# Query, key and value products of a DiT block by seven products, with the MLP's weight pieces in unused memory

## The chip, the cores and the metric

One core of one Trainium2 chip runs the whole block as one program. The metric is the device time of one execution in microseconds, lower is better; the time before is the median of three runs, 2368.72 us (2368.39 to 2368.92).

The engines are named as the profile names them: PE is TensorE (matrix products; PEld its weight loads), DVE is VectorE, ACT is ScalarE, POOL is GpSimd, and SP is SyncE, which here only issues DMAs. Each engine takes its instructions in the order in which the built program lists them; an instruction that waits holds all behind it on that engine.

## The reference, cut to what matters

A DiT block in fp32 for two sequences ("rows", B=2) of T=2048 tokens, width D=512, 16 heads of 32, hidden width 2048. A condition vector gives six vectors of shift, scale and gate.

```python
mod = silu(condition) @ Wada + bada
sh_a, sc_a, gt_a, sh_m, sc_m, gt_m = split(mod, 6, axis=1)
xm = layernorm(x, g1, be1) * (1 + sc_a) + sh_a
qkv = (xm @ Wqkv).reshape(b, t, 3, H, hd).transpose(2, 0, 3, 1, 4)
scores = einsum("bhqd,bhkd->bhqk", q, k) * hd**-0.5     # causal, softmax
x = x + gt_a * (attn @ Wproj + bproj)
xm = layernorm(x, g2, be2) * (1 + sc_m) + sh_m
x = x + gt_m * (gelu(xm @ W1 + b1) @ W2 + b2)
```

The change concerns the product xm @ Wqkv, and the preparation of W1 and W2 for the MLP.

## The kernel before, in words

**Stages.** In order of time (span of the profiled execution): the query, key and value stage ("Qkv") of row 0 to about 213 us; its attention to 755; its projection to 812, in which the LayerNorm and the transposes of row 1's first tokens are made; the Qkv stage of row 1 from 812 to about 1004; its attention; its projection from about 1546 to 1607; and the MLP of both rows to the end at 2365.

**A Qkv stage** goes over four groups of 512 tokens (`Qkv.group`, L801 on). xmT holds the group's normalised and modulated tokens, transposed: 512 channels as four chunks of 128 partitions, by 512 tokens. For each of four chunks f of 128 outputs, first of the queries and then of the keys, four matmuls (one for each channel chunk, contraction 128, 512 columns; L203) fill one PSUM bank. There are six such banks ("mm"). An fp32 matmul is two passes in the trace. The scores of the attention need a query or key as a high part and a residue, both fp32r: ScalarE writes the scaled high part, hl[:,0] (L821), VectorE the residue hl[:,1] = scaled product − hl[:,0] (L822), and SyncE stores both to DRAM in one DMA of 512 KB (L827). hl has four buffers in row 0, three in row 1. After f=0 the four key loads and four query loads of the group (256 KB each, L305 to L325) follow on SyncE; kst is one tile for all four groups. Then come four value tiles: four matmuls of 512 columns each, copied by ScalarE (L843) into vv, which stays on chip.

**What is put between.** After each of the twelve output tiles, `between(n)` issues the rest: the load of the next group's x (n=0), its LayerNorm and transposes (n=5 and 8: VectorE normalises into xn, L244; TensorE transposes, L211; VectorE modulates even chunks, L263, and ScalarE odd ones, L268), and `also(g, n)`. Within the matmuls `among` brings scores of the attention's first three units forward in groups 1 to 3: TensorE fills one of two banks "s", VectorE takes the row maximum (L461, or L456 where the causal mask applies).

**What sets the order.** Instructions wrapped in `mm()` or `act()` stay in program order; the tile scheduler may move the others. All DMAs of `nc.sync` go through SyncE's queue in order, and with at most eight outstanding there. In row 0, `also` loads the modulation's weights ("wada", L1050): for two of the six vectors at a time, eight DMAs of 256 KB on SyncE, in group 0 and in group 1.

**The MLP's weights.** The MLP already multiplies by seven products in place of eight (a form of Strassen's scheme, with halves of contraction, outputs and tokens), which needs sums of weight blocks. `Quarters` (L876 to L950) makes them during the Qkv stages, all on GpSimd: it issues the loads of a piece of W1 or W2 (L929, L942), adds blocks (L913) and stores the piece to DRAM (L902). There are eight W1 pieces (seven blocks of 128x256: four sums) and four W2 pieces (eight sums, of 512 and 896 columns, then seven stores). Their memory is that of wada in row 0 and a tile of its own in row 1.

Of the kernel before, what the change touches and what calls it, by code (L numbers as in the profile page):

```python
# [27 lines left out]
def dit_block_kernel(  # L28
# [119 lines left out]
    rstd2 = const.tile([P, B * NT], F32, tag="rstd2", name="rstd2")  # L148
    shift2 = const.tile([P, B * NT], F32, tag="shift2", name="shift2")
# [70 lines left out]
    def inv_std(mv, rstd, lo, hi):  # L220
        nc.scalar.activation(rstd[:, lo:hi], mv[:, lo:hi, 1], AF.Sqrt, bias=eps)
        nc.vector.reciprocal(rstd[:, lo:hi], rstd[:, lo:hi])

# [6 lines left out]
    def transposed(pool_, psum, xts, n0, mv, rstd, a, c, b, dst, xns=None):  # L230
# [28 lines left out]
        def modulate(chunks=range(C)):  # L259
            for k in chunks:  # L260
                src = banks[k // per][:, k % per, :]
                if k % 2 == 0 and not by_act:
                    nc.vector.tensor_scalar(  # L263
                        dst[:, k, :], src,
                        a[:, k, b : b + 1], c[:, k, b : b + 1], ALU.mult, ALU.add,
                    )
                else:
                    nc.scalar.activation(  # L268
                        dst[:, k, :], src, AF.Identity,
                        bias=c[:, k, b : b + 1], scale=a[:, k, b : b + 1],  # L270
                    )
# [17 lines left out]
    class Row:  # L289
# [18 lines left out]
        def load_keys(self, c, g, n=1):  # L308

            tok = slice(g * MT, (g + n) * MT)  # L310
            if g == 0:
                self.kst[c] = self.pools[c % 2].tile(
                    [P, HC, T], F32R, tag=f"kst{c % 2}", name="kst"
                )
            for r in range(4):
                nc.sync.dma_start(
                    self.kst[c][r * HD : (r + 1) * HD, :, tok].bitcast(F32),
                    kd[self.b][c][r % 2, :, tok].rearrange("(h d) t -> d h t", d=HD),
                )
# [65 lines left out]
        def prefetch(self):  # L385
# [6 lines left out]
            st = bp.tile([P, HC, T], F32R, tag="kst0", name="kst")  # L392
            st = st.bitcast(F32).rearrange("p h t -> p (h t)")
            self.at_s = [
                st[:, n * C * QB : (n + 1) * C * QB].rearrange("p (c q) -> p c q", c=C)
                for n in range(2)
            ]
            self.xt_s = [st[:, (2 * C + n) * QB : (2 * C + n + 1) * QB] for n in range(TQ)]
            self.wproj = st[:, 3 * C * QB :].rearrange("p (c d) -> p c d", c=C)
# [42 lines left out]
        def bank(self, u, h, t, kb, s):  # L442
# [6 lines left out]
                self.kst[c][:, h, kb * QB : kb * QB + w],  # L449
# [86 lines left out]
    def attention_phase(row):  # L536
        b, vv, kst, qst = row.b, row.vv, row.kst, row.qst
        with pool(f"att{b}") as ap, pool(
# [6 lines left out]
            def scores_t(u, step, n):  # L545
# [29 lines left out]
                for h in range(HC):  # L575
                    at = 0
                    for j, q in tiles:
                        mm(
                            sts[h][:, at : at + QB - q],
                            kst[c][:, h, j * P : (j + 1) * P],  # L580
# [178 lines left out]

    class Qkv:  # L760


        def __init__(self, row, qp, psum):
            self.row, self.qp, self.psum = row, qp, psum
            self.xts, self.xmT = {}, {}
            self.w = qp.tile([P, C, 3 * D], F32, tag="wqkv", name="wqkv")
# [9 lines left out]
        def load_w(self, queue):  # L776
            w_v = Wqkv.rearrange("(c p) f -> p c f", p=P)
            for f in range(0, 3 * D, D):
                act(queue.dma_start(self.w[:, :, f : f + D], w_v[:, :, f : f + D]))

        def stats(self, g, t, keep=False):
# [3 lines left out]
            if t == MTT - 1:  # L785
                inv_std(mv1, rstd1, n0, n0 + MTT)

        def norm(self, g, j):

            b = self.row.b  # L790
            if j == 0:
# [3 lines left out]
                self.xmT[g] = self.qp.tile([P, C, MT], F32, tag="xmT", name="xmT", bufs=2)  # L795
            return transposed(
                self.qp, self.psum, self.xts[g][2 * j : 2 * j + 2],
                b * NT + g * MTT + 2 * j, mv1, rstd1, a1, c1, b,
                self.xmT[g][:, :, j * 2 * P : (j + 1) * 2 * P],
            )  # L800

        def group(self, g, hp, between, among):


            row, w, psum = self.row, self.w, self.psum
            b, xmT = row.b, self.xmT[g]
            tok = slice(g * MT, (g + 1) * MT)
            n = 0
            for f in range(C):
                for which in range(2):  # L810
                    ps = psum.tile([P, MT], F32, tag="mm", name="ps_qk")
                    w0 = which * D + f * P
                    for k in range(C):
                        mm(
                            ps, w[:, k, w0 : w0 + P], xmT[:, k, :],
                            start=(k == 0), stop=(k == C - 1),
                        )
                        among(n, k)
                    hl = hp.tile([P, 2, MT], F32R, tag="hl", name="hl", bufs=4 - b)
                    scale = HD**-0.5 if which == 0 else 1.0  # L820
                    nc.scalar.activation(hl[:, 0, :], ps, AF.Copy, scale=scale)  # L821
                    nc.vector.scalar_tensor_tensor(  # L822
                        hl[:, 1, :], ps, scale, hl[:, 0, :].bitcast(F32),
                        ALU.mult, ALU.subtract,
                    )
                    dst = (qd if which == 0 else kd)[b][f]
                    nc.sync.dma_start(  # L827
                        dst[:, :, tok].rearrange("l p t -> p l t"), hl.bitcast(F32)
                    )
                    between(n)  # L830
                    n += 1
                if f == 0:
                    row.load_keys(0, g)
                    row.load_queries(g)
            for t in range(MTT):
                ps = psum.tile([P, D], F32, tag="mm", name="ps_v")
                for k in range(C):
                    mm(
                        ps, xmT[:, k, t * P : (t + 1) * P], w[:, k, 2 * D : 3 * D],
                        start=(k == 0), stop=(k == C - 1),  # L840
                    )
                    among(n, k)
                nc.scalar.copy(row.vv[:, g * MTT + t, :], ps)  # L843
                between(n)
                n += 1

        def run(self, hp, also):

            row = self.row
            for g in range(NG):  # L850

                def between(n):
                    if g + 1 < NG:
                        if n == 0 and g + 1 not in self.xts:
                            self.load_x(g + 1)
                        if n in (5, 8):
                            self.norm(g + 1, n // 8)()
                    elif n == 8:

                        row.rows(0)  # L860
                        act(nc.scalar.activation(first, eps, AF.Exp))
                    also(g, n)

                def among(n, k):
                    if g > 0 and n >= 2:


                        past = 4 * (n - 2) + k + 1
                        if g == 1:
                            row.score(row.count(cum[0] * past / 40, 0))  # L870
                        else:
                            past += 40 * (g - 2)
                            row.score(
                                row.count(
                                    cum[0] + (cum[2] - cum[0]) * past / 80,
                                    1 if g == 2 and n < 7 else 2,  # L876
# [3 lines left out]
                self.group(g, hp, between, among)  # L880

    w1_v = W1.rearrange("(c p) f -> p c f", p=P)
    w2_v = W2.rearrange("(c p) f -> p c f", p=P)

    piece = 7 * C // 2 * P
    S1, S2, A11, S4, A12, A22, S3 = range(7)
    A21 = S4

    class Quarters:

# [5 lines left out]
        def __init__(self):  # L896
            self.rooms, self.more_rooms, self.at = [], None, 0
            self.to = []

        def store(self):  # L900
            for dst, w in self.to:
                nc.gpsimd.dma_start(dst, w)  # L902
            self.to = []

        def sums(self, part):

            for n, x, y, op in (
                (S1, A21, A22, ALU.add),
                (S3, A11, A21, ALU.subtract),
                (S2, S1, A11, ALU.subtract),  # L910
                (S4, A12, S2, ALU.subtract),
            ):
                nc.gpsimd.tensor_tensor(part(n), part(x), part(y), op)  # L913

        def step(self):

            self.store()
            f, self.at = self.at, self.at + 1
            if f >= FC // 2 + C:
                return  # L920
            if not self.rooms:
                self.rooms = self.more_rooms()
            w = self.rooms.pop(0)
            base = ((A11, 0, 0), (A12, 0, 1), (A21, 1, 0), (A22, 1, 1))
            if f < FC // 2:
                w = w[:, :piece].rearrange("p (n c d) -> p n c d", n=7, d=P)
                for n, i, k in base:
                    at = (f + i * FC // 2) * P
                    nc.gpsimd.dma_start(  # L929
                        w[:, n],  # L930
                        w1_v[:, k * C // 2 : (k + 1) * C // 2, at : at + P],
                    )
                self.sums(lambda n: w[:, n])
                self.to = [(w1d[f], w)]
                return
# [803 lines left out]
```

## Time and profile before

| | |
|---|---|
| Median of three runs | 2368.72 us (2368.39 to 2368.92) |
| Profiled execution: time, span | 2366.88 us, 2365.2 us |
| Granted TensorE clock | 1.000 |
| Qkv stage, row 0: groups | 17.9 to 60.98 to 108.56 to 162.79 to about 213 us |
| Qkv stage, row 1: groups | 812.2 to 855.3 to 902.3 to 953.7 to about 1004 us |
| Busy VectorE in row 0's groups | 12.9, 21.5, 35.8, 30.8 us |
| Busy GpSimd in row 1's groups | 27.1, 27.4, 30.8, 18.5 us |

The profile gives one execution. Its first part has the busy time of each engine. The chain is the work that ended last, followed back from the end, each step to what released it; in order of time it shows runs of one kind of instruction with their start and length. Groups of instructions show engine, output and inputs, shape, count, then busy time, mean of one in ns, and the idle time before them with its releaser. A window of a stage lists the busy time of each engine in it. A stretch of SyncE's queue shows when DMAs were issued. The mean of a matmul in a group (594 ns) counts ends that overlap the next; what one adds to the chain is read from the chain.

### The profile page before, as it was taken

Reading aid. Unit: us, or ns where it says so; the run is one execution under the profiler, and the core shown is the slowest. Engines: PE = TensorE matmul, PEld = TensorE weight load, DVE = VectorE, ACT = ScalarE, POOL = GpSimd, SP = SyncE. Lnnn points to the kernel's source line nnn. Section 1 sums busy time; section 2 is a strip of 40 time slices with the busy share of each in tenths; the row PEclk is TensorE's granted clock in tenths of the full one; section 3 lists DMA queues with packets and bytes.
Section 4 is the critical chain, followed back from the end, with each engine's and each line's share of the span. In section 5 each row is a group of like instructions: output and inputs, shape, how many; then the busy total and the mean of one; then the engine's idle time right before and its main releaser. Section 6 shows DMA issues by size and latency. Waiting matters only on the chain.

```text
span 2365.2 us, 32348 instructions
## 1 busy us (share of the span) xinstructions
PE 2336.9 (99%) x11469; PEld 1294.6 (55%) x11469; DVE 1397.6 (59%) x2868; ACT 924.1 (39%) x1736; POOL 1079.2 (46%) x1219
## 2 busy tenths in 40 slices
PE   8999999999999999999999999999999999999998
PEld 4455555555544445555555555444585486487477
DVE  3466666767656636576666766553483374365356
ACT  2113555555555012155555555613322332332321
POOL 1052997978793646379887997460000000000000
PEclk9999999999999999999999999999999999999999
DMA  7577215151223788650513214272254254353433
GB/s 258 188 249 195 49 28 118 27 117 46 83 106 132 255 259 259 220 113 24 117 46 85 59 31 144 78 252 100 98 170 146 94 179 139 119 166 132 135 124 129
DMA packets 134106, 311.49 MB, mean 132 GB/s; under 512 B 14208, under 2 KB 29100, under 8 KB 129080
## 3 DMA queue, kind: packets, MB, share of 16 engines
q1 hardware_dynamic: 126096, 277.13, 38.9%
q0 software_dynamic: 7472, 31.75, 3.7%
q8 instruction: 90, 1.47, 0.3%
q14 instruction: 72, 0.59, 0.1%
q10 hardware_dynamic: 376, 0.55, 0.1%
HBM read 229.95 MB, written 87.29 MB: 134 GB/s over the span
## 4 chain that ended last, share of the span: by engine, by line
PE 96%; DVE 2%; POOL 1%; issue 0%; DMA 0%; ACT 0%; SPq 0%; POOLq 0%; ACTq 0%; DVEq 0%
PE st L203 20%; PE ps_a L203 17%; PE o L203 11%; PE s L203 10%; PE ps_qk L203 9%; PE ps_b L203 9%; PE ps_v L203 5%; PE ps_o L203 5%; PE ps_c L203 4%; PE sm L203 4%; PE ps_xt L211 1%; POOL ee L614 1%; PE ps_o L211 1%; DVE mx L461 0%; DVE junk L456 0%
## 5 line engine op out<-in xcount | busy, mean ns | idle before, releaser
L586 ACT ACTIVATE e<-st 128x512 f32<-128x512 f32 (+1 forms) x1152 | 574.6, 578 | 428.1 <-PE st L203 361.6
L614 POOL TENSOR_TENSOR ee<-ee,e 128x512 f32<-128x512 f32 x424 | 529.2, 1289 | 4.4 <-ACT e L586 4.0
L461 DVE TENSOR_REDUCE mx<-s 128x1 f32<-128x512 f32 x604 | 407.9, 688 | 204.5 <-PE s L203 203.1
L203 PE MATMUL s<-kst,qst 128*128 128x512 f32 (+3 forms) x1032 | 463.7, 451 | 5.7 <-DVE mx L461 2.9
L203 PE MATMUL st<-qst,kst 128*128 128x512 f32 (+3 forms) x1280 | 409.4, 387 | 0.0
L203 PE MATMUL ps_a<-sum,w 128*128 128x256 f32 (+1 forms) x1088 | 346.6, 454 | 0.0
L203 PE MATMUL o<-e,vv 128*32 128x512 f32 (+3 forms) x2560 | 300.5, 538 | 2.0 <-POOL e L592 2.0
L456 DVE CUSTOM_DVE_ANT_0 junk<-s,causal 128x512 bf16<-128x512 f32 (+3 forms) x428 | 209.3, 489 | 135.5 <-PE s L203 127.6
L203 PEld LDWEIGHTS s<-kst,qst 128*128 128x128 f32 x1032 | 194.4, 189 | 155.7 <-DVE mx L461 55.6
L203 PEld LDWEIGHTS st<-qst,kst 128*128 128x128 f32 x1280 | 227.3, 188 | 94.2 <-issue 62.2
L203 PEld LDWEIGHTS ps_a<-sum,w 128*128 128x128 f32 x1088 | 206.3, 190 | 109.8 <-issue 91.4
L614 POOL TENSOR_TENSOR ee<-e 128x512 f32<-128x512 f32 x168 | 210.4, 1285 | 101.4 <-ACT e L586 101.0
L203 PE MATMUL ps_qk<-xmT,wqkv 128*128 128x512 f32 x512 | 239.0, 594 | 1.8 <-DVE xmT L263 1.8
L592 POOL TENSOR_SCALAR_AFFINE_SELECT e<-e 128x128 f32<-128x128 f32 (+1 forms) x384 | 122.4, 357 | 135.0 <-ACT e L586 132.3
L203 PE MATMUL st<-fold,sel 32*128 32x512 f32 (+1 forms) x1152 | 149.1, 481 | 0.9 <-ACT vv L843 0.5
L203 PEld LDWEIGHTS ps_qk<-xmT,wqkv 128*128 128x128 f32 x512 | 93.9, 190 | 97.0 <-issue 90.4
L1318 DVE TENSOR_TENSOR h<-c,ps_b 128x512 f32<-128x512 f32 x32 | 22.0, 687 | 202.4 <-PE ps_b L203 202.4
L203 PEld LDWEIGHTS st<-fold,sel 32*128 32x128 f32 x1152 | 59.3, 181 | 144.8 <-ACT e L586 86.6
L203 PE MATMUL ps_v<-wqkv,xmT 128*128 128x512 f32 x256 | 122.3, 594 | 0.0
L203 PE MATMUL ps_b<-sum,w 128*128 128x256 f32 (+1 forms) x384 | 120.6, 450 | 0.0
L203 PEld LDWEIGHTS o<-e,vv 128*32 128x32 f32 x2560 | 61.1, 108 | 102.0 <-issue 81.0
L1492 ACT ACTIVATE h<-h,cols 128x512 f32<-128x512 f32 x96 | 69.2, 721 | 118.6 <-DVE h L1318 118.6
(155 smaller groups left out, 2601.3 us busy)
## 6 DMA issues: line engine op xcount, KB each, us to landing
qst<-q SPq DMA_DIRECT2D x128, 256.0 KB
w<-w1d SPq DMA_DIRECT2D x32, 896.0 KB
w<-w2d SPq DMA_DIRECT2D x28, 1024.0 KB
kst<-k SPq DMA_DIRECT2D x24, 1024.0 KB
w<-w2d SPq DMA_DIRECT2D x28, 768.0 KB
q<-hl SPq DMA_DIRECT2D x32, 512.0 KB
k<-hl SPq DMA_DIRECT2D x32, 512.0 KB
w2d<-w POOLq DMA_DIRECT2D x28, 448.0 KB, 6.5
```

The costliest lines, as they stand in the source:

```text
L203: return tc.keep_in_program_order(nc.tensor.matmul(*args, **kw))
L211: return tc.keep_in_program_order(nc.tensor.transpose(dst, src, ident[:n, :n]))
L456: nc.vector.tensor_tensor_reduce(junk[:, :w], s[:, :w], causal[:, QB - w :], 1.0, MASKED, ALU.add, ALU.max, m,)
L461: nc.vector.tensor_reduce(m, s[:, :w], axis=AX.X, op=ALU.max)
L586: act(nc.scalar.activation(e[:, :w], sts[h][:, :w], AF.Exp))
L592: nc.gpsimd.affine_select(d, d, pattern=[[0, len(tiles)], [1, P]], compare_op=ALU.is_ge, fill=0.0, base=0, channel_multiplier=-1,)
L614: act(engine.tensor_tensor(dst, x, y, ALU.add))
L1318: act(nc.vector.tensor_tensor(dst, x, y, ALU.add))
L1492: nc.scalar.activation(d, ps, AF.Gelu, bias=col(r_b1 + half * HF + f, 1))
```

## The change

**Queries and keys by seven products.** For a group and an f, the query chunk and the key chunk are the two halves of the outputs (i = 0, 1), channel chunks 0-1 and 2-3 the halves of the contraction, and tokens 0-255 and 256-511 the halves of the tokens. The four products of halves come from seven block products, each two matmuls of 256 columns; the weights and tokens of four of these are sums (S1 to S4). Banks a, b and c collect them:

```diff
+            return [
+                step("a", A11, True, first, 0, 0),
+                step("b", S1, True, first, 1, 1),
+                step("a", S2, False, first, 0, 1),
+                step("b", S4, False, last, 0, 1),
+                step("c", A12, True, last, 0, 0),
+                step("a", S3, False, last, 1, 1),
+                step("a", A22, False, direct, 1, 0),
+            ]
```

`first` copies a bank into hl[:,1] on ScalarE (128x256), `last` adds a bank to it on VectorE, and `direct` is a copy that completes the key. The last step of a unit is issued after the second of the next unit:

```diff
+                    for step in steps[:2] + late + steps[2:6]:
+                        step()
+                        tick()
+                    late = steps[6:]
```

Then the chunk is split into high part and residue, on ScalarE and GpSimd, before SyncE stores it:

```diff
-                    hl = hp.tile([P, 2, MT], F32R, tag="hl", name="hl", bufs=4 - b)
-                    nc.scalar.activation(hl[:, 0, :], ps, AF.Copy, scale=scale)
-                    nc.vector.scalar_tensor_tensor(
-                        hl[:, 1, :], ps, scale, hl[:, 0, :].bitcast(F32),
-                        ALU.mult, ALU.subtract,
-                    )
...
+                hp.tile([P, 2, MT], F32R, tag="hl", name="hl", bufs=4) for _ in range(2)
...
+            def split(i):
+                hl = hls[i]
+                d = hl[:, 1].bitcast(F32)
+                nc.scalar.copy(hl[:, 0], d)
+                nc.gpsimd.tensor_tensor(hl[:, 1], d, hl[:, 0].bitcast(F32), ALU.subtract)
+                self.stored(g, f, i, hl)
```

**Values** are two units a group by the same seven products with the same token sums: the tokens are the weights of TensorE there, the value weights' seven blocks (256 columns) move; `first` and `last` copy and add into vv. A group is thus six units of seven products, and `tick` is called after each product (42 a group). Only unit (0, 0) of row 0 is computed as before (`plain`).

**Sums.** Token sums S1, S2, S3 (ticks 36, 38, 40 of the group before) and A22 (tick 2) are VectorE operations of 128x512 in place in xmT or in three new tiles. Weight sums of queries and keys: GpSimd in row 0, sixteen of 128x256; in row 1 three of 128x1024 on VectorE and one on GpSimd, during the projection. Value weights: four of 128x512 on GpSimd, in each row's first group (tick 10 in row 1).

**LayerNorm.** xn is now made by ScalarE in place in the x tile, with a new vector `shift1`, and modulation is ScalarE's too, but for row 0's first group. x of the next group is loaded at tick 3; its norm is at ticks 18 and 28.

**MLP pieces** (`Pieces` for `Quarters`): loads go through SyncE's queue; sums and stores are queued and taken by ticks, on GpSimd still; the memory is that of vv, kst and qst that is not used yet. `plan(f, room, load, start)` gives the ticks, counted through the stage:

```diff
+        def tick(self):
+            for f in self.events.pop(self.at, ()):
+                f()
+            self.at += 1
+            for _ in range(2 if len(self.ops) > 12 else 1):
+                if self.ops:
+                    self.ops.pop(0)()
...
+        pieces.plan(FC // 2, room_2, 5, 17)
+        for f, (room, load, start) in enumerate((
+            (room_v, 4, 12), (room_v, 25, 36), (room_v, 46, 54), (room_k, 56, 63),
+            (room_q, 66, 73), (room_k, 80, 87), (room_q, 91, 98), (room_k, 105, 112),
+        )):
+            pieces.plan(f, room, load, start)
...
+            for f, (room, load, start) in enumerate((
+                (room_2, 0, 6), (room_1, 16, 24), (room_2, 39, 46),
+            ), FC // 2 + 1):
+                pieces.plan(f, room, load, start)
```

Row 0 so takes one W2 piece and the eight W1 pieces, row 1 the other three W2 pieces. A W2 piece in `room_2` lies in four parts of memory, so its eight sums are twenty operations: four of 512 columns, twelve of 256, four of 128; the seven stores are one step, taken by one tick.

**Other moves.** wada has its memory in vv; its eight DMAs in group 0 are issued at tick 7. kst is a tile for each group, so the attention's key loads of 1 MB become four of 256 KB each. The MLP's computation is not changed.

## The prediction

> **What bounds the kernel now.** I read the page's busy row first, then the shares of the chain, then the costliest groups.
>
> ```profile
> PE 2336.9 (99%) x11469; PEld 1294.6 (55%) x11469; DVE 1397.6 (59%) x2868; ACT 924.1 (39%) x1736; POOL 1079.2 (46%) x1219
> PE 96%; DVE 2%; POOL 1%; issue 0%; DMA 0%; ACT 0%; SPq 0%; POOLq 0%; ACTq 0%; DVEq 0%
> ...
> L203 PE MATMUL ps_qk<-xmT,wqkv 128*128 128x512 f32 x512 | 239.0, 594 | 1.8 <-DVE xmT L263 1.8
> ...
> L203 PE MATMUL ps_v<-wqkv,xmT 128*128 128x512 f32 x256 | 122.3, 594 | 0.0
> ```
>
> TensorE is busy 99% of the span and carries 96% of the chain, at a granted clock of 1.00 everywhere: work taken off it is time gained, unless it then waits. The two lines are the passes that the change touches, 512 + 256 = 768 (two for each fp32 matmul). Their mean, 594 ns, is the modelled end of overlapping passes; the chain in order of time gives what one costs:
>
> ```profile
> 812.22 20.60 PE ps_qk L203 x48
> ...
> 860.66 4.55 DMA x<-in_x_dram
> ```
>
> 48 passes in 20.60 us are 0.429 each. A pass of 256 columns costs 0.216 (the MLP's seven products: 8 in 1.73 us, in the same view), so halving the columns halves the cost. The second line is the only stall: in the second group of batch row 1 the next group's x landed late and TensorE stood for 1.2 us. So the present order has much cover, and the question is how much of it the change uses up. The busy times of the stages tell it (us, PE, PEld, DVE, ACT, POOL, clock, DMA share, GB/s); first two groups of row 0, then of row 1:
>
> ```profile
> 17.90:60.98 43.08, 43.05 (x112) 20.00 (x113) 12.91 (x27) 11.12 (x20) 0.16 (x1) 1.00 0.70 224
> 60.98:108.56 47.58, 47.58 (x146) 22.61 (x144) 21.54 (x62) 9.75 (x18) 0.00 (x0) 1.00 0.65 210
> ...
> 812.20:855.30 43.10, 43.10 (x114) 19.97 (x113) 15.37 (x32) 8.90 (x18) 27.08 (x32) 1.00 0.82 271
> 855.30:902.30 47.00, 45.78 (x129) 22.16 (x128) 22.88 (x59) 9.02 (x17) 27.35 (x27) 1.00 0.84 264
> ```
>
> GpSimd does nothing in row 0's first two groups and 27 us in row 1's. No query, key or value waits for it anywhere, since it only makes MLP weight pieces. That is what the change gives up.
>
> **TensorE's gain.** A group is 96 passes now, 96 × 0.429 = 41.2 us. After: six units of seven products, each two matmuls of two passes, 168 × 0.216 = 36.3: −4.9. The very first unit stays plain (16 × 0.429 + 140 × 0.216 = 37.1): −4.1. Over eight groups 7 × 4.9 + 4.1 = **−38.2 us**, if nothing waits.
>
> **Vector and scalar engines.** VectorE loses, a group, eight residues (0.687), four normalisations (0.55) and four modulations (0.54), and gains 18 adds of 256 columns (0.42, the MLP's rows) and four token sums (0.61, half of the 1.22 for 1024 columns): −0.2 us, so 13 to 36 us of a group as before. ScalarE goes to about 22 us of 39 to 49. Both are covered. What may not be is order: a late operation ahead of an add in VectorE's queue holds TensorE (it does, below).
>
> **GpSimd.** Its rates:
>
> ```profile
> L913 POOL TENSOR_TENSOR w<-w 128x256 f32<-128x256 f32 x32 | 23.2, 735 | 10.6 <-DMA w<-in_L_cond_W_dram 9.5
> ...
> L913 POOL TENSOR_TENSOR w<-w 128x512 f32<-128x512 f32 x16 | 20.2, 1264 | 19.4 <-DMA w<-in_L_cond_W_dram 18.6
> L902 POOL DMA_DIRECT2D w2d<-w x28 | 15.2, 548 | 1.2 <-POOL w L913 1.2
> ```
>
> Start to start they are 0.72 and 1.22, a store's issue 0.55. After the change the residue of each query and key chunk (the split, 128x512, 1.22) is taken on this engine, eight a group, in program order behind whatever the ticks have queued. A tick is one product, 4 × 0.216 = 0.86 us: each tick that queues a sum of 1.22, or two operations while more than twelve stand, puts GpSimd further behind. A split that is late makes its store late, the store frees one of four hl tiles, and the next unit's first product can't be copied out without a tile; its PSUM bank takes the third product, so TensorE stops there, two or three products later. From a store's issue to the load that depends on it SyncE's queue shows 3.4 to 6.1 us (26.59 to 30.0, 172.04 to 178.18).
>
> A W2 piece costs GpSimd four sums of 512 (4.9), twelve of 256 (8.6), four of 128 (0.5 each, below the 256 row: 2.0) and seven stores (3.9): 19.4 us, where the sums went in eight wider operations before. Row 1 adds three such pieces in its first two groups (58.2), 16 splits (19.5), the value weights' sums (4.9) and loads (4 × 0.72): **85.5 us**, starting 3.5 us in. TensorE's own work there is 36.3 + 1.7 of transposes, and 2.9 of scores more in the second group: 38 + 41 = 79 us; it took 90.1 before. So in these two groups GpSimd is the busier engine, and the splits stand in its line. Walking the queue in program order from 812.1: the second unit's splits end at T+24.8 and T+29.5, and with 4 us for a store to land the waits at third and fourth products are 3.5 + 4.9 + 3.8 = 12 us; the third piece, begun four ticks into the next group, gives 5.6 + 2.0 = 7.5. The bounds: 0 (tiles are never short, as now) and 24 (6.1 us to land, everywhere).
>
> **Row 0, first group.** Two waits, one inside the other. First SyncE:
>
> ```profile
> 34.37 0.38 SPq L827 DMA_DIRECT2D q<-hl  x1
> 34.79 5.86 SPq L1050 DMA_DIRECT2D wada<-in_L_cond_Wada_dram  x6
> 41.45 0.38 SPq L827 DMA_DIRECT2D k<-hl  x1
> ```
>
> The key chunk, ready at 33.3, was stored at 41.45 because six loads of modulation weights stood ahead, 0.98 us each; there were tiles to spare. Now the second unit's query store stands behind all eight, and loads of MLP pieces are on this queue as well (they were on GpSimd's): issued about 44, landed 47 to 50, where the fourth unit wants the tile at 37.8: some 10 us. Second, GpSimd: from 18.1 us, 29 sums of 256 (20.9), 8 sums and 4 splits of 512 (14.6) and four issues (2.2) stand up to the store of W2's third part: 55.8 us. It lands 6.5 later (the median of the 28 in the page's DMA list, 2.8 to 13.3), at 62.3; a W1 load into the same memory waits for it on SyncE's queue, with two loads of the next group's x behind it; these land near 66, and their statistics stand ahead of the fifth unit's value adds on VectorE. TensorE goes on at about 68.4 with 5.3 us to do: the group ends at 73.7 instead of 60.98 − 4.1 = 56.9. **+16.8**; it is 13 with a landing of 2.8, 24 with 13.3, and 0 if pieces and x never meet.
>
> The Trainium skill ("DMA: Bandwidth & Descriptors", Anatomy of one DMA — SWDGE path) has a store as a fixed 2.0 us and its bytes at 436 GB/s: 3.1 us for 448 KB, against 6.5 here, where several queues move at once. By the page this group's wait would be 13.4, and the sum 3.4 us lower.
>
> **Row 0, second group.** The eight modulation loads took 83.01 to 91.2 on SyncE; a key store again comes behind them and one unit later there is no tile: 6.5 us (0 to 10).
>
> **Third and fourth groups.** W1 pieces only (3.4 us each), GpSimd at a third: no wait taken, 0 to 3 a row.
>
> **Attention, projection, MLP.** Sixteen key loads of 256 KB in place of four of 1 MB, on a queue with long gaps there; six operations on VectorE in projection 0 under TensorE's 57 us. Taken at nothing; without that cover 1 to 3 us.
>
> VectorE and GpSimd at once:
>
> ```profile
> L244 DVE TENSOR_SCALAR xn<-x,mv,rstd x28: 534/545/2301, 7.6 to 928.1; 128x512 f32<-128x512 f32 x28
> ...
> L244 DVE TENSOR_SCALAR xn<-qst,mv,rstd x12: 514/1008/4846, 773.8 to 1592.2; 128x512 f32<-128x512 f32 x12
> ```
>
> (min/median/max): 0.55 alone, up to 4.8 beside GpSimd. These go to ScalarE, but four token sums a group come, and the splits run beside them; 0 to 1 us each on the way to the next group, taken at nothing. "SBUF — State Buffer", Who interferes with whom, says that an operation with two SBUF inputs and a reading GpSimd lock each other out entirely: by it the token sums would lose a split's length each, some 1.2 us, 30 us over the kernel if none were covered; no row here shows that form.
>
> **Sum.** −38.2 + 16.8 + 6.5 + 12 + 7.5 = **+4.6 us**. The profiled execution took 2366.88 (span 2365.2), so 2371.5 by it; on the median of 2368.72, 2373.3. Forecast: **2373 us**. A measurement of this kernel tells 0.2% (4.7 us) from no change.
>
> **Rivals.**
> - *The waits are half as long*: stores land in 3 us, SyncE's modulation loads go out faster since half of the bytes asked for then are gone from GpSimd's queue, and the walk stacked waits that overlap. 21 us of waits, −17: about 2352. For it: stalls that I added one after another; every late store of before (41.45, 91.31) did no harm. Against: four tiles with two taken by each unit.
> - *Nothing waits*: 2368.72 − 38.2 = 2330.5. The 1.2 us stall in all of before's eight groups speaks for it; GpSimd's 85.5 us in 79 against it.
> - *Slower, by GpSimd's line alone*: if its operations are stretched by VectorE at its side (the split's row may go from 1.22 to 1.48, as the slowest 128x512 group on that engine shows), row 1's two groups hold 85.5 × 1.15 = 98 us, 8 to 13 more, and row 0's first 6 more: about 2390. It decides as soon as GpSimd's work in those groups exceeds TensorE's by more than the four tiles hold, one unit, 6 us.
>
> **How the numbers follow.** Waits of 36 to 50 us (2366 to 2380) 0.41; half 0.27; nothing 0.08; slower by GpSimd's line 0.24. Of the first case a half lies within 0.2%. Faster 0.36, same 0.20, slower 0.44. Range 2344 to 2393: both bounds of the row 0 landing and the half case lie in it; all of the gain doesn't. The likeliest case alone: 2366 to 2380.
>
> **What would show it.** In the changed kernel's profile: 1316 passes of 256 columns at 0.216; the first group ending near 73, the groups at 812 near 50 us each, with TensorE's idle time released by the copy into hl (ScalarE), behind it a store; GpSimd near 85 us of those two groups; the last two groups of each row 5 us shorter. If the first group ends before 61, or the pair at 812 takes under 85, the waits are smaller than worked out and the kernel is faster; if GpSimd's 128x512 rows exceed 1.4 us, it is slower.

## The result, and the profile after

The changed kernel takes 2426.82 us (median of 4 runs, 2425.97 to 2428.19) against 2368.82 (4 runs): a ratio of 1.0245, 95% interval 1.0227 to 1.0263. It is 58 us slower, where no change to speak of was forecast, and outside the range.

The busy row, the shares of the chain and the granted clock, from the page of the changed kernel:

```profile
PE 2326.1 (96%) x12033; PEld 1413.6 (58%) x12033; DVE 1404.1 (58%) x2930; ACT 1009.9 (42%) x1952; POOL 1147.5 (47%) x1291
...
PEclk9899999999999988999999999999999999999999
...
PE 82%; DMA 5%; POOL 5%; issue 3%; DVE 2%; SPq 1%; ACT 1%; POOLq 0%; DVEq 0%; ACTq 0%
```

TensorE's busy time fell by only 11 us, its share of the chain from 96% to 82%, and DMA, which held nothing of the chain, now holds 5%. The clock dips twice, in the slices of the two Qkv stages. Span by span (us):

| | before | after |
|---|---|---|
| up to the first query product | 17.9 | 19.5 |
| Qkv stage, row 0 | 194.5 | 220.7 |
| attention 0 | 542.4 | 542.0 |
| projection 0 | 57.2 | 58.6 |
| Qkv stage, row 1 | 191.2 | 221.4 |
| the rest, to the end of the span | 1361.9 | 1362.5 |

Of the 59.5 us in span, 56.4 lie in the two stages, which should each have become 19 us shorter if nothing waited. The windows of their first two groups (columns as in the prediction: us, PE, PEld, DVE, ACT, POOL, clock, DMA share, GB/s; row 0, then row 1):

```profile
19.50:79.90 60.40, 41.43 (x168) 31.11 (x169) 22.79 (x46) 23.85 (x50) 51.42 (x64) 0.89 0.92 304
79.90:138.60 58.70, 46.67 (x218) 38.74 (x217) 21.92 (x67) 20.38 (x45) 20.94 (x24) 0.85 0.73 244
```

```profile
840.80:904.40 63.60, 47.15 (x181) 38.41 (x180) 15.57 (x38) 20.07 (x45) 55.58 (x67) 0.84 0.76 249
904.40:964.10 59.70, 47.37 (x201) 40.39 (x200) 20.76 (x66) 20.27 (x45) 28.86 (x36) 0.83 0.60 204
```

TensorE stands idle 12 to 19 us in each, and what it does runs at a mean clock of 0.83 to 0.89. Who held it is read from one operation, the copy of a bank into an hl tile on ScalarE (L938): what ScalarE waited for before it, and which engine then waited for the copy (us, times). The second view is of the kernel before: who waited for its stores of queries and keys.

```profile
its engine sat idle before it (us, times) until:
...
  DMA q<-hl: 27.2, 8
  DMA k<-hl: 24.5, 9
...
who waited for it (us, times):
...
  PE ps_a L204: 37.6, 10
...
  PE ps_b L204: 18.8, 5
```

```profile
L827 SPq DMA_DIRECT2D k<-hl x32: 359/377/863, 26.6 to 996.7; - x32
...
who waited for it (us, times):
  ACT hl L821: 4.0, 1
```

ScalarE's copies stood 51.7 us for stores, where they stood 4.0 before, and TensorE stood 56.4 us for the copies: TensorE waits for the copy, the copy for a tile, the tile for a store.

### The profile page after: what moved, and what is told of

It reads as the page before. It is cut to its first block, busy times and chain, and to the rows that moved or that the text cites. A ratio compares the mean times of both kernels' runs of the same rounds, so it can differ in the third digit from the quotient of the medians.

```text
span 2424.7 us, 34152 instructions
## 1 busy us (share of the span) xinstructions
PE 2326.1 (96%) x12033; PEld 1413.6 (58%) x12033; DVE 1404.1 (58%) x2930; ACT 1009.9 (42%) x1952; POOL 1147.5 (47%) x1291
## 4 chain that ended last, share of the span: by engine, by line
PE 82%; DMA 5%; POOL 5%; issue 3%; DVE 2%; SPq 1%; ACT 1%; POOLq 0%; DVEq 0%; ACTq 0%
PE ps_a L204 20%; PE st L204 19%; PE o L204 11%; PE ps_b L204 10%; PE s L204 9%; PE ps_c L204 5%; PE sm L204 4%; PE ps_o L204 3%; DMA k<-hl 2%; DMA q<-hl 1%; POOL kst L1123 1%; POOL hl L944 1%; PE ps_xt L212 1%; POOL ee L621 1%; DVE mx L468 1%
## 5 line engine op out<-in xcount | busy, mean ns | idle before, releaser
L204 PE MATMUL s<-kst,qst 128*128 128x512 f32 (+3 forms) x1032 | 419.1, 410 | 6.8 <-DVE mx L468 6.3
L944 POOL TENSOR_TENSOR hl<-hl 128x512 fp32r<-128x512 f32 x62 | 78.8, 1270 | 198.8 <-ACT hl L943 166.6
L468 DVE TENSOR_REDUCE mx<-st 128x1 f32<-128x512 f32 x164 | 112.6, 687 | 4.1 <-PE st L204 1.3
L204 PE MATMUL ps_a<-t,wqk 128*128 128x256 f32 x248 | 67.2, 400 | 39.3 <-ACT hl L938 37.4
```

Of the source, the lines that this page charges most:

```text
L204: return tc.keep_in_program_order(nc.tensor.matmul(*args, **kw))
L468: nc.vector.tensor_reduce(m, s[:, :w], axis=AX.X, op=ALU.max)
L944: nc.gpsimd.tensor_tensor(hl[:, 1], d, hl[:, 0].bitcast(F32), ALU.subtract)
```

## The experiments

Row 0 and row 1 below are the lengths of the two Qkv stages; idle is TensorE's in each (from the waits in its queue). Times are of one run, but for the first two kernels and six; the kernel before took 2367.7 to 2368.4 on the same chips.

| | time | row 0 (idle) | row 1 (idle) |
|---|---|---|---|
| before | 2368.8 | 194.5 (0) | 191.2 (1.2) |
| changed | 2426.8 | 220.7 (35) | 221.4 (32) |
| split_vector | 2422.8 | 229.2 (38) | 208.5 (27) |
| wada_spread | 2423.4 | 217.0 (28) | 219.8 (33) |
| comb | 2409.3 | 218.4 (29) | 206.5 (25) |
| comb2 | 2409.7 | 212.4 (22) | 210.6 (26) |
| wv_four | 2427.5 | 219.2 (31) | 224.0 (39) |
| wv_seven | 2394.5 | 203.3 (17) | 205.1 (27) |
| spare_only | 2405.8 | 207.5 (22) | 213.0 (33) |
| fix | 2408.0 | 216.5 (27) | 206.2 (25) |
| wv_seven_x | 2360.8 | 192.5 (11) | 184.2 (10) |
| wv_seven_all | 2359.9 | 186.6 (3) | 188.0 (11) |
| x_ahead | 2420.0 | 219.9 (34) | 214.6 (29) |
| mixed | 2405.2 | 216.4 (24) | 203.3 (17) |
| six | 2370.7 | 197.9 (12) | 187.5 (10) |
| old_two | 2386.8 | 199.9 (4) | 205.0 (10) |

### The two queues that the prediction named

**split_vector:** the residue is made on VectorE.

```diff
-                nc.gpsimd.tensor_tensor(hl[:, 1], d, hl[:, 0].bitcast(F32), ALU.subtract)
+                nc.vector.tensor_tensor(hl[:, 1], d, hl[:, 0].bitcast(F32), ALU.subtract)
```

> Theory A (GpSimd's line): the split of a query or key chunk stands in GpSimd's queue behind the MLP pieces' sums, so its store, and with it the hl tile that the next unit's first copy wants, comes late. With the split on VectorE, nothing of a query or key waits for GpSimd: row 1's Qkv stage goes from 221 to about 185 us, row 0's (where SyncE's modulation loads hold the stores as well) from 221 to about 212, the time from 2427 to about 2382. Theory B (the seven-product form itself: more copies, adds and one chain over two banks, whoever makes the residue): the stages keep their length within 10 us, 2417 to 2437, since VectorE gets 8 x 0.69 us a group more.

Measured: 2422.8, in the range of theory B. Row 1's stage became 13 us shorter where theory A had 36, and row 0's 8.5 longer. GpSimd no longer touches a query or key, and the copies still wait 48.8 us for stores (51.7 in the changed kernel). Theory A is a part of row 1's loss, not the whole. Some stores of row 1 now stood on SyncE; this is the one behind the longest wait there (SyncE's queue, and two pieces of the chain):

```profile
918.70 4.12 DMA k<-hl
...
922.84 4.51 SPq L319 DMA_DIRECT2D kst<-k  x4
...
930.14 8.17 DMA q<-hl
```

A query chunk was ready at 921.4 us, but its store was issued at 930.1: ahead of it on SyncE stood the attention's key and query loads, and the first key load waited for the group's first key store to land. TensorE then waited 8.4 us for that tile. No run moves these loads, so what they cost is open.

**wada_spread:** the modulation loads one at a time.

```diff
...
+            if todo and n % 3 == 0:
+                todo.pop(0)()
```

> The sixteen modulation loads of row 0 are issued one at a time, every third tick, in place of eight at once. Theory C (SyncE's line): in row 0's first two groups the stores stand behind the eight loads (10.3 and 11.6 us of SyncE); without them the 15.3 us wait in the first group goes to under 5 and the 4.5 and 7.5 us waits in the second to under 3; row 0's Qkv stage goes from 221 to about 198 us, row 1's stays at 221, the time is about 2404. If only GpSimd's line counts (theory A alone), row 0's stage stays above 215 and the time above 2420.

Measured: 2423.4, with row 0's stage at 217.0, the signs that were named for GpSimd's line alone. The 15.3 us wait of the first group went to 9.0, but a wait of 1.6 us for a value add became 6.8; the waits on stores went from 51.7 to 40.9. Theory C missed by 19 us.

**comb**, both, with `g < 2` choosing VectorE, and **comb2**, with the W2 piece of row 0 a group later:

> Both edits, with the split on VectorE in the first two groups of a row and on GpSimd in the last two. Theories A and C together: row 0's stage about 185 us, row 1's about 183, no wait on a store over 2 us, granted clock 1.00, time about 2352. If the waits have a further source (DMA bandwidth in row 0's first group, share 0.92; order on ScalarE), one of the stages stays above 195 us and the time above 2365.

> As the kernel with both edits, and the W2 piece of row 0 is moved from the first group to the second (its loads at tick 38, its sums from tick 46), with the W1 pieces behind it. If the W2 piece's loads, stores and sums in the first group still cost something after the other two edits, row 0's stage is 3 to 8 us shorter than there; if not, the two agree within 2 us.

Measured: 2409.3 and 2409.7; waits on stores in comb still 42.6 us. comb gains more than the sum of the two alone (17.5 us against 7.5; the split is on GpSimd again in the last two groups here), and is 57 short of what both theories together promised. In comb2 row 0's stage is 6.0 us shorter than in comb, as was expected if the W2 piece costs something there; but row 1's stage, whose code is the same in both, is 4.1 longer, and the times agree. A stage with the same code can so differ by 4 us, and single gains of that size in the table show little. The two queues are then a part of the loss, 17.5 of 58 us: with one late link mended, the next took its place. What they all feed is the hl tile, and the next runs ask whether it has too little slack.

### Tile life

**wv_four** and **wv_seven** leave out the value weights (the value products read the query weights, so the values are not the reference's) and so free memory; only the second gives it to hl:

```diff
     def load_wv(self, hp, queue):
-            self.wv = hp.tile([P, 7, HK, D // 2], F32, tag="wv", name="wv")
...
+            self.wv = self.w[:, :, :, : D // 2]
...
-                hp.tile([P, 2, MT], F32R, tag="hl", name="hl", bufs=4) for _ in range(2)
+                hp.tile([P, 2, MT], F32R, tag="hl", name="hl", bufs=7) for _ in range(2)
```

> Control. The value weights' tile, its loads and its sums are left out: the value products read the query weights instead, so the values are not those of the reference; the work on TensorE, VectorE and ScalarE is the same, GpSimd loses 4.9 us a row and SyncE four loads. hl keeps four tiles. Every theory: between 2412 and 2425 us, the waits of ScalarE's first copy on stores (51.7 us in the changed kernel) above 40.

> The same with the memory so freed given to hl: seven tiles in place of four, nothing else. Theory D (tile life): in the changed kernel an hl tile is taken at a unit's first product and is the place where products are added up, so it is held through a unit (6 to 8 us) before its store starts; four tiles are two units, which leaves about 4 us for the split, SyncE and the landing, and every store that takes longer is a wait of TensorE. With seven tiles the waits on stores fall from 50 to under 12 us, the granted clock in the stages rises to 0.97 or more, and the time is 50 to 70 us below the control, about 2355. Theory B (the form itself, or engines in the unit's chain): within 15 us of the control, above 2400.

Measured: 2427.5 and 2394.5. The control lies 2.5 us above its range and within 1 us of the changed kernel; its copies wait 39.6 us for stores. Three tiles more are worth 33 us. TensorE's waits in row 1's stage and its surroundings (total, times, longest), wv_four and then wv_seven:

```profile
PE ps_a L204 <- ACT hl L929: 27.1, 5, 9.8
PE ps_b L204 <- ACT hl L929: 6.5, 2, 4.9
PE ps_a L204 <- ACT vv L1000: 4.8, 1, 4.8
```

```profile
PE ps_xt L212 <- ACT x L844: 19.8, 4, 17.4
PE ps_a L204 <- ACT hl L929: 4.6, 1, 4.6
PE ps_a L204 <- DVE vv L1004: 2.9, 2, 2.3
```

The waits on hl go from 33.6 us to 4.6; in both stages together ScalarE's copy no longer lists a store of queries or keys among its releasers. But more than half of that is given back at once: a wait of 17.4 us for the transposes of the next group's x appears, and the gain is short of the expected 50 to 70 us. TensorE now gets ahead of x, and x is late by two things. Its loads landed at 892.5 us, 5.4 after TensorE stopped; then a VectorE instruction on the way to the normalisation, of 0.17 us in the median, took 9.28:

```profile
894.32 9.28 DVE L224 SCALAR_TENSOR_TENSOR shift<-mv,rstd 128x4 f32<-128x4 f32 x1
...
901.63 1.94 POOL L1114 TENSOR_TENSOR qst<-qst 128x256 f32<-128x256 f32 x4
```

All that time GpSimd ran one operation on on-chip tiles after another, and both ended at the same moment, 903.6 us. This points to VectorE being held by GpSimd; no run shows it by taking GpSimd's work away.

**old_two:** the kernel before with two tiles.

```diff
-                    hl = hp.tile([P, 2, MT], F32R, tag="hl", name="hl", bufs=4 - b)
+                    hl = hp.tile([P, 2, MT], F32R, tag="hl", name="hl", bufs=2)
```

> The kernel before with two hl tiles in each row in place of four and three, nothing else. There a tile is held for the two halves (0.60 + 0.69 us) and its store; a chunk comes every 3.4 us, so two tiles leave some 5.5 us for a store against 15 and 10 now. Theory D: stores of 4 to 8 us then hold the copies, and with six PSUM banks in between TensorE waits some, 5 to 40 us over both stages, 2374 to 2410. If a store's wait does not reach TensorE: within 4 us of 2368.

Measured: 2386.8, +18 us, within the expected range. ScalarE's copies waited 72.4 us for stores, 27 times, more than in the changed kernel, and TensorE was idle 14 us against 67: so there a store's wait reaches TensorE much less. From the program, the reason would be that a chunk is complete in its bank and six banks stand between, while in the seven products the third product needs the first one's bank back; no run tests that by itself.

### x, with and without tiles

**wv_seven_x** adds to wv_seven, and **x_ahead** to the changed kernel:

```diff
...
+                        if n == 30 and g + 2 < NG:
+                            self.load_x(g + 2)
+                        if n in (8, 10, 12, 14) and g + 1 > row.b:
+                            self.stats(g + 1, (n - 8) // 2, True)
+                        if n in (15, 25):
+                            self.normalise(g + 1, n // 25)
```

> The kernel with the value weights left out (values not the reference's) and seven hl tiles, and x earlier: the next group's x is loaded at tick 30 of the group before in place of tick 3, its statistics are held in program order at ticks 8 to 14, its normalisation is issued three ticks ahead of the transposes. Theory E (x's line): with tiles to spare, what is left are waits of TensorE for transposes of an x that is late on SyncE, and for adds that stand on VectorE behind its statistics, 17.4 + 6.2 + 3.2 + 2.3 + 1.8 + 1.5 us in the kernel with seven tiles. They go: time 2352 to 2368. Theory B (the form itself): within 10 us of 2394.

> The changed kernel (full computation, four tiles) with x earlier as there, nothing else. Theory D: tiles bound it first, so the time falls by the waits on value adds alone (1.6 + 5.9 us) or less: 2412 to 2425. If x's line is the main cause, it falls by 30 us or more, below 2397.

Measured: 2360.8 and 2420.0, both as theories E and D had them. The same edit is worth 34 us with seven tiles and 7 with four. Theory B, that the form itself is slow, is out: with tiles and an early x it runs 8 us below the kernel before. The edit also moves the statistics to another time, and no VectorE instruction is held for 9 us any more, so the 34 us are not divided between x's loads and GpSimd's hold. **wv_seven_all** (with comb's two edits) asks for the rank of the queues:

> The same, with the split on VectorE in the first two groups of a row and the modulation loads one at a time. Theories A and C as lesser causes that seven tiles cover: within 8 us of the kernel without these two edits, either way. If GpSimd's and SyncE's lines still hold stores back: 10 to 20 us less, 2340 to 2350.

Measured: 2359.9, no difference from wv_seven_x: with tiles to spare, the split's engine and the modulation loads cost nothing in sum (row 0's stage is 5.9 us shorter, row 1's 3.8 longer). **fix** and **spare_only**, the full computation with eight tiles in the first two groups, came too early for this:

> Full computation. In the first two groups of a row every second unit takes its two hl tiles from the key memory of the third and fourth group, which is unused then: eight tiles there. The MLP pieces leave that memory: row 0 makes the eight W1 pieces only, row 1 the four W2 pieces. Split on GpSimd, modulation loads eight at once. Theory D: the waits on stores in the first two groups fall to a third, those of the last two groups stay (1 to 3 us each); time 2365 to 2395. If GpSimd's and SyncE's lines are what counts (theories A and C), it stays above 2400.

> Eight hl tiles in the first two groups as there, and the split on VectorE in those groups, the modulation loads one at a time, and the statistics of the next group's x kept in program order, so that on VectorE they no longer stand ahead of the value adds (waits of 1.6 to 6.8 us there). Theory D with A and C as lesser causes: both Qkv stages between 175 and 186 us, granted clock 0.99 or more, time 2335 to 2350, below the kernel before. Theory B: above 2395.

Measured: 2405.8 and 2408.0; both missed, and on the side of the other theories. spare_only won 21 us, 11 less than its range asks, and lies above the 2400 named for theories A and C. One wait is more than that difference: at 951.9 us TensorE had stood 16.9 us for a tile. On SyncE a load of the next W2 piece had waited 18.8 us for the store of the piece before it from the same memory, with stores of keys and queries behind it. So eight tiles do not cover a queue that is held that long. fix lies 58 us above its range, where theory B was expected. In it, statistics were put in order at the tick of the transposes themselves; TensorE waited 5 to 7 us for x five times (43.2, 91.4, 145.1, 900.3 and 958.1 us), and row 0's third query load waited for a piece stored from its memory. These waits are 30 us, and some 40 with the 1.9 us lost after each (an estimate from the rows further down): most of the miss is that edit's, as far as can be told without a run that takes it back alone.

**mixed** gives tiles their room in another way:

> Full computation: queries and keys by seven products, values plain again (which frees 6 KB a partition, S3 gets its own tile), hl five tiles, x earlier, split on VectorE in the first two groups, modulation loads one at a time. TensorE's gain is 8 x (27.5 - 24.2) = 26 us. With five tiles of the seven needed, waits of 10 to 25 us remain: time 2352 to 2372. If five tiles do as little as four, above 2385.

Measured: 2405.2, 33 us above the range's end, and where five tiles were expected if they do as little as four. With five tiles there are waits of 7.0, 6.9 and 6.3 us on hl again: an odd fifth tile may help little where they are taken in pairs, which was not tried by itself.

**six:** the full computation with more tiles and an early x, and with comb's two edits, so it does not part tiles from queues.

```diff
...
+            if g < 2 and (g * C + f) % 3 == 2:
+                hls = [self.spare[:, :2], self.spare[:, 2:]]
```

> Full computation. One pair of hl tiles more in the first two groups of a row (the key memory of the fourth group), so six there and four in the last two; x earlier; split on VectorE in the first two groups (row 1: three), modulation loads one at a time; MLP pieces in what memory is left, each loaded when the piece before it should have landed. Theories D and E carry over: waits on stores under 10 us in the first two groups, 4 to 8 us in the last two; TensorE idle under 30 us in both stages (67 in the changed kernel); time 2362 to 2382. If the cause lay in the value weights that were left out, above 2400.

Measured: 2370.7 us (10 runs), a ratio of 1.0011 to the kernel before, interval 1.0001 to 1.0020: 56 us below the changed kernel, within the range expected. TensorE's waits for value copies, hl and x in row 0's stage:

```profile
PE ps_a L204 <- ACT vv L1018: 4.6, 1, 4.6
PE ps_a L204 <- ACT hl L945: 3.9, 2, 2.1
...
PE ps_b L204 <- ACT hl L945: 1.7, 1, 1.7
PE ps_xt L212 <- ACT x L847: 1.2, 3, 0.4
```

So what mended the kernel without value weights mends the full one. No version of the full computation beat the kernel before.

## Why the prediction was wrong

The sum had +4.6 us and the kernel lost 58. The chain of waits was the one foretold; three sizes in the sum were wrong: TensorE's gain (10 us too large), the length of the waits (66 us of additional idle time against 42.8) and what a wait costs after it has ended (some 17 us, taken at nothing).

**TensorE's gain, −38.2.** Too large by some 10 us even without waits. Busy TensorE in both stages: 384.5 us before, 356.1 in wv_seven_x, 28.4 less, at clocks of 0.99. A pass of 256 columns in the chain is 0.214 to 0.219 (fourth group of row 0 in wv_seven), as predicted; a score pass between them went from 0.210 to 0.229 (wv_seven) in the fourth group of row 0. For the 192 score passes of both stages that would be 3.6 us, an estimate. The rest of the difference was not separated.

**The waits, 42.8 us, against 94.8 lost.** Per group, the loss is the measured span less the old span and its gain (first group: 60.4 − (43.1 − 4.1) = 21.4):

| | g0 | g1 | g2 | g3 |
|---|---|---|---|---|
| row 0: predicted | 16.8 | 6.5 | 0 | 0 |
| row 0: lost | 21.4 | 16.0 | 2.1 | 5.4 |
| row 1: predicted | 12 | 7.5 | 0 | 0 |
| row 1: lost | 25.4 | 17.6 | 2.2 | 4.7 |

−38.2 + 94.8 + 1.6 (start) + 1.4 (projection) comes to 59.6, and the spans differ by 59.5. Of the 94.8, 66 us are idle TensorE and 28 a longer busy time than the sum's, which has in it the 10 us of the gain. The places were right: first groups worst, last ones nearly free. Three steps failed.

1. *The step "A split that is late makes its store late, the store frees one of four hl tiles".* The chain was right, but the margin of the four tiles was never worked out. An hl tile used to be taken when a chunk was complete (0.60 + 0.69 us, then the store). Now it is where the products are added up. From the changed kernel's own rows: a product takes 0.87 us; a key tile is taken at the end of the second product and complete at the end of the tenth (eight products, 7.0 us), then come copy, high part and residue (0.38 + 0.62 + 1.27), so 9.2 us pass before its store can start; a query tile, done with the sixth product, takes about 6.7. Four tiles are two units of seven products, 12.1 us. That leaves 2.9 us for a key's store and 5.4 for a query's, and 1.7 more until the bank is wanted again; landings in the chain were 3.6 to 8.6 us, once 11.9. So a long landing holds TensorE even when no queue is late, and any lateness of a queue adds to it at once; I priced two queues and took the tiles for cover. This is the term that wv_seven (−33) and old_two show.

2. *"Third and fourth groups ... no wait taken", and x, seen in one place.* The last two groups of both rows held 7.3 us of idle time, 6.1 of it for hl, so step 1 again. Of x the prediction had "their statistics stand ahead of the fifth unit's value adds on VectorE" in row 0's first group alone; the wait was 1.6 us there, and 5.9 in row 1's first group, where none was priced. An earlier x is worth 7 us in the changed kernel, and 34 once tiles are there.

3. *A stall was priced at its length.* It cost more. Rows of TensorE around two waits of the changed kernel, the first after 15.27 us (start, length with a modelled end, count, wait):

```profile
59.35 2.07 PE L204 MATMUL ps_a<-t,wqk 128*128 128x256 f32 x4 [15.27 <-ACT hl L938]
61.22 1.97 PE L204 MATMUL ps_b<-xmT,wqk 128*128 128x256 f32 x4
62.98 1.07 PE L204 MATMUL ps_c<-xmT,wqk 128*128 128x256 f32 x4
63.89 1.03 PE L204 MATMUL ps_a<-xmT,wqk 128*128 128x256 f32 x4
...
168.91 1.13 PE L204 MATMUL ps_a<-t,wqk 128*128 128x256 f32 x4 [0.99 <-ACT hl L938]
```

From start to start the first four passes took 1.87 us, the next four 1.76, the third 0.91: half speed for 3.6 us, 1.9 us lost. After the wait of 0.99 us there is none of it. Busy TensorE of the changed kernel is 374.4 us, 28 above the sum's 346.3; eight or nine such waits at 1.9 us are some 17, most of what is not in the 10 us above.

**GpSimd's line.** Its load was right: 84.4 us (55.6 + 28.9) in row 1's first two groups against 85.5. That the splits stand in its line was right too. There 13 of the 16 splits began 1.0 to 15.7 us after their high part was ready, and in row 0's first group four began 2.7 to 9.4 late; in the last two groups of both rows it was under 0.4. One of them, from ScalarE's and GpSimd's queues, and the group of all splits:

```profile
853.39 0.62 ACT L943 CAST hl<-hl 128x512 fp32r<-128x512 f32 x1 [1.73 <-DVE hl L950]
...
868.54 1.26 POOL L944 TENSOR_TENSOR hl<-hl 128x512 fp32r<-128x512 f32 x1
...
L944 POOL TENSOR_TENSOR hl<-hl 128x512 fp32r<-128x512 f32 x62 | 78.8, 1270 | 198.8 <-ACT hl L943 166.6 <-issue 28.8 <-DMA kst<-k 3.2
```

TensorE's waits for hl in row 1's first two groups come to 22.9 us, against 19.5 priced, so this term was nearly right in size. With the split on VectorE there, row 1's stage was 11 to 15 us shorter (split_vector, comb, comb2), and with seven tiles nothing was left to gain. The rival "slower, by GpSimd's line alone" had the sign and not the mechanism: a split took 1.27 us in the mean, not its 1.48, and row 0's second group, where no split was late, lost 16.0 us all the same.

**SyncE's line.** The eight loads in row 0's first group took 10.3 us, not 8:

```profile
40.38 10.30 SPq L1263 DMA_DIRECT2D vv<-in_L_cond_Wada_dram  x8
52.17 0.38 SPq L910 DMA_DIRECT2D q<-hl  x1
```

The store went out at 52.2 and not at 44, and landed at 58.8; the wait was 15.3, not 10. The size was off, the mechanism right, and yet its removal won 3.4 us: other waits grew, as told under wada_spread.

**VectorE beside GpSimd**, taken at nothing. The token sums (32 of them, so the 30 us of the prediction should be 39 at 1.2 us each), in the changed kernel's row 0 stage, have means of 0.78, 1.02 and 0.85 us in their three forms, against 0.68 for the fastest: 16 sums, some 2.8 us more. In row 1 one took 6.05 us, with GpSimd busy for 5.62 of them, in the projection before the stage. The Trainium skill ("SBUF — State Buffer", Who interferes with whom) has such pairs shut each other out. The traces agree in single cases (this one, and the 9.28 us in wv_seven), but most sums lost far less than a split's length. VectorE's balance in the prediction has its sign wrong: it loses 9.9 us a group and gains 10.0, which changed nothing.

**"Nothing waits"** (2330) has no counterpart: the nearest, wv_seven_all, has 14 us of idle TensorE left and 2359.9 us.

## What to carry to other kernels

When a buffer becomes an accumulator, work out its life anew: from its first write to the landing of its store, against the number of buffers times the time between takings. A late queue costs time where it is later than that margin, and then mending one queue shows only a part, because the next late link waits behind it; work out the margin first and look at the queues after. Price a stall of the matrix engine above its length, and check what an engine made faster will reach next (here x).

## What the runs showed of the hardware

After waits of TensorE of 4 us or more, the first four passes of 256 columns showed 1.7 to 2.1 us in all kernels where such passes follow directly, against 1.03 in flow; after a wait of 0.6 to 3.2 us they mostly showed 1.1, and the exceptions there mostly come shortly after another wait; between 3.2 and 4 us both are seen. The Trainium skill ("TensorE: Matmul & The Clock Gate", Part 1, the HAM clock gate) says the same: the array falls to half its clock after an idle window of about 3.4 us and needs about as much activity to come back; the runs agree, with 3.6 us of half speed after the 15.27 us wait. The groups' clock follows: 0.83 to 0.89 in groups with long waits, 1.00 in the last two groups of each row.
